# Graph attention and residual norm in float32: every product of the slots in four 64 by 64 tiles of TensorE, and the norms' statistics on ScalarE

## The chip, the cores and the metric

The kernel runs on one core of a Trainium2 chip. Its time is the device time of one execution in microseconds (us), the median of several runs. A core has a matrix engine (PE in the profile; PEld is its weight load), a vector engine (DVE), ScalarE (ACT), GpSimd (POOL) and SyncE (SP), which here issues most of the loads and stores. [...]

## The reference

Two layers on x of 8 batch elements, 2048 nodes and 256 features, with a symmetric 0/1 matrix adj of 2048 by 2048, four heads of 64.

```python
# layer 0
q, k, v = (x @ W.T + b, per head, for Wq, Wk, Wv)
scores = clip(q @ k.T / 8, -10, 10);  scores[adj == 0] = -10
attn = softmax over each chunk of 256 columns, 8 chunks        # not over all 2048
ctx = sum over the chunks of attn @ v
y = layernorm(ctx @ Wo.T + bo + x) * gamma + beta
x = layernorm(x + y)
# layer 1
Wh = x @ W;  e = leaky_relu(Wh @ a_src (rows) + Wh @ a_dst (columns), 0.2)
e[adj == 0] = -inf;  alpha = softmax(e) over all columns
x = layernorm(x + elu(alpha @ Wh))
```

All of it is in float32. There are three norms in an element: the inner norm of layer 0 (called a in the kernel), the outer one (b) and the one that closes layer 1 (c).

## The kernel before

Scores are made transposed, with columns j of the adjacency on the 128 partitions and 512 rows i along the free axis (CH = 512, so four groups q of rows). An element's layer 0 is cut into 64 **slots**: slot s is a group of rows q, a pair of heads hp and a chunk c of 256 columns. In a slot:

- `scores` makes four matmuls, for two blocks u of 128 columns and two heads k. Each head has 64 of the 128 rows of TensorE, so the two heads of a block run at once in two tiles of 64 by 128 (L385). They go to ps, two banks of PSUM in turn (`two_banks`, pool psA). DVE clips them and takes the mask, both in one instruction: the lesser of the score and the slab's byte, plus or minus 80 (L396). The slab is loaded three slots ahead.
- `exps`: ScalarE's exponential in place (L408).
- `product(s, k)`: for one head, attention times values, extended by a column of ones for the softmax's sum. One matmul is 128 rows by 64 columns of TensorE with 65 streamed columns (L422), and the two halves z of a block run at once in two column tiles. ScalarE copies the result out (L429).
- `normalize`: DVE's reciprocal (L437), GpSimd's multiply and add into acc (L444, L446).

While element b does layer 0, element b - 1 does **layer 1** in the same slots, in `Layer1.step`. The unit of layer 1 is half of the rows (BANKS = 8, 8 blocks of 128) and a head. A tile of it is 128 columns j by 1024 rows i: DVE makes e from the row factors srow, the column factor gd and the edge bytes et (`make`, L741), PE multiplies it into pa (`use`, L763, tiles of 128 by 64 again). A slot has two tiles (STEP = 2), made two ahead in three buffers.

The order on every engine is written out by hand (`manual_schedule`). In slot s, PE gets scores(s + 1), product(s, 0), layer 1's tiles, product(s, 1). DVE gets the reciprocal of slot s - 1, the clips of s + 1, then e. When a group of rows is finished, its output, two norms and projection to layer 1 (`Between`) are laid over the 16 slots of the next group by tables: AHEAD, BESIDE and BEHIND, and WIDE_... for the two middle groups. The number is the slot in the group; "beside" steps stand between the scores and the product, "behind" steps after the slot's work. `output` (L537) and `values` (L581, the projection, one block of 128 nodes at a time) are 128 by 128 matmuls, and they use a bank of their own, psM. The closing norm of element b - 2 (`Closing`) lies over the first 16 slots in the same way, and the last two elements have tables for the end, CLOSING_ALONE and ENDING.

```python
def stats(self, ks):                       # a norm's statistics, all on DVE
    for k in ks: nc.vector.bn_stats(...); nc.vector.bn_aggr(...)
    rs = var + EPS; off = -mean            # DVE
    rs = rs ** -0.5; off = off * rs        # GpSimd
def apply(self, dst):                      # ScalarE, L502
    dst = Identity(rs * src + off)         # four, of 256 columns
```

Between two elements stands a stretch in which the next element's x is projected to q, k and v (L329, L345) and the last group's `Between` is done in one go. `factors` then makes layer 1's row and column factors, and `rows` stores the row factors to rowD. After the last element, layer 1 runs alone (64 steps).

## Time and profile before

| | |
|---|---|
| median of 3 runs | 3774.59 us (3774.26 to 3775.82) |
| profiled execution | 3776.29 us, its span 3774.5 us |
| granted TensorE clock, mean | 0.993 of full speed |
| instructions in the span | 159,666 |
| DVE e (L741) | 1024 of 1286 ns |
| DVE pr (L396) | 1024 of 1207 ns |
| ACT exps (L408) | 1024 of 1055 ns |
| PE records of L422, L763, L385 | 32,768, 32,768, 4096 |

The page of the profile gives an engine's busy time, share of the span and instructions; then, for each line and operation, the tiles written and read, their shapes and count, the busy time, the mean duration and what the engine waited for before. "Busy" of a group is the time in which at least one of its instructions ran beyond the engine's earlier ones, so it is less than count times duration where they overlap. On PE every float32 matmul stands as two records, and each has a record of a weight load.

### The profile page before, as it was taken

To read this page: it belongs to the slowest core of one execution; us is meant where nothing else is said; L and a number is where in the kernel's file an instruction comes from. 1 tells how busy PE (TensorE), PEld (TensorE's weight loads), DVE (VectorE), ACT (ScalarE), POOL (GpSimd) and SP (SyncE) were. 2 spreads that over 40 slices of the span, in tenths; PEclk is the share of its full clock that TensorE was granted. 3 is DMA by queue.
4 is the path that set the end of the run, shared out by engine and by line. 5 is a ranking of instruction groups with operands and counts; after the bars stand their busy time and mean duration, and the time that the engine had idled before them with its cause. 6 is when DMAs were issued, how large, how long until landed. Compare 5 with 4: busy or idle time off the path is not lost.

```text
span 3774.5 us, 159666 instructions
## 1 busy us (share of the span) xinstructions
PE 3664.0 (97%) x72100; PEld 2741.3 (73%) x72100; DVE 3133.7 (83%) x4202; ACT 1988.0 (53%) x3665; POOL 1365.5 (36%) x1202
## 2 busy tenths in 40 slices
PE   9999999999999999999999999999999999999786
PEld 5656677776777777776777767777677777776676
DVE  5877489986999689895998959988699977988798
ACT  4666455555555555555555545555455555555322
POOL 1445234333433343333443324433334333334300
PEclk9999999999999999999999999999999999999998
DMA  6652333333333343333433334333433333433354
GB/s 163 152 117 69 78 98 109 105 75 112 106 108 105 86 119 102 104 93 88 133 97 98 100 89 135 109 100 78 113 107 107 105 80 112 115 97 84 95 154 128
DMA packets 672060, 398.46 MB, mean 106 GB/s; under 512 B 427280, under 2 KB 591504, under 8 KB 671376
## 3 DMA queue, kind: packets, MB, share of 16 engines
q1 hardware_dynamic: 621376, 354.54, 35.6%
q10 hardware_dynamic: 50000, 33.70, 2.8%
q8 instruction: 564, 9.24, 1.0%
q14 instruction: 120, 0.98, 0.1%
HBM read 331.22 MB, written 56.89 MB: 103 GB/s over the span
## 4 chain that ended last, share of the span: by engine, by line
PE 86%; DVE 5%; issue 3%; ACT 3%; DMA 1%; POOL 1%; SPq 0%; ACTq 0%; DVEq 0%; POOLq 0%
PE pc L422 26%; PE ps L385 24%; PE pa L763 22%; PE pp L329 5%; PE po L537 3%; PE pw L581 3%; PE pv L345 2%; DVE e L741 2%; ACT y L502 1%; DVE pr L396 1%; ACT pr L408 1%; DMA xp<-in_x_dram 0%; PE pm L246 0%; ACT qT L337 0%; SPq L279 0%
## 5 line engine op out<-in xcount | busy, mean ns | idle before, releaser
L396 DVE SCALAR_TENSOR_TENSOR pr<-ps,slab 128x1024 f32<-128x1024 f32 x1024 | 1194.3, 1207 | 211.1 <-PE ps L385 207.7
L422 PEld LDWEIGHTS pc<-vaug,pr 128*64 128x64 f32 x32768 | 1039.5, 138 | 406.4 <-issue 313.6
L741 DVE SCALAR_TENSOR_TENSOR e<-srow,gd,et 128x1024 f32<-128x1024 f32 x1024 | 1273.1, 1286 | 10.4 <-PE pa L763 5.8
L422 PE MATMUL pc<-vaug,pr 128*64 128x65 f32 x32768 | 1155.9, 224 | 14.3 <-ACT raw L429 7.7
L763 PE MATMUL pa<-waug,e 128*64 128x65 f32 x32768 | 1069.8, 224 | 41.0 <-DVE e L741 36.4
L763 PEld LDWEIGHTS pa<-waug,e 128*64 128x64 f32 x32768 | 1015.1, 139 | 60.1 <-DVE e L741 45.5
L408 ACT ACTIVATE pr<-pr 128x1024 f32<-128x1024 f32 x1024 | 1038.2, 1055 | 32.8 <-DVE pr L396 26.4
L385 PE MATMUL ps<-qT,kT 64*128 64x512 f32 x4096 | 1023.2, 616 | 3.5 <-DVE pr L396 2.9
L429 ACT COPY raw<-pc 128x260 f32<-128x260 f32 x1024 | 380.5, 372 | 1222.7 <-PE pc L422 1178.7
L444 POOL TENSOR_TENSOR part<-raw,rd 128x512 f32<-128x512 f32 x448 | 467.9, 1044 | 1407.5 <-DVE rd L437 1389.4
L446 POOL TENSOR_TENSOR acc<-acc,part 128x512 f32<-128x512 f32 x448 | 575.0, 1283 | 35.2
L385 PEld LDWEIGHTS ps<-qT,kT 64*128 64x128 f32 x4096 | 349.9, 186 | 326.6 <-issue 229.6
L437 DVE RECIPROCAL rd<-raw 128x8 f32<-128x8 f32 x512 | 100.8, 197 | 132.1 <-ACT raw L429 129.6
L444 POOL TENSOR_TENSOR acc<-raw,rd 128x512 f32<-128x512 f32 x64 | 66.7, 1043 | 339.3 <-DVE rd L437 339.3
L581 PE MATMUL pw<-w_sb,x1T 128*128 128x264 f32 x512 | 139.8, 409 | 6.1 <-DVE x1T L291 5.0
L795 ACT ACTIVATE sums<-sums,dn 128x64 f32<-128x64 f32 x512 | 134.0, 337 | 9.7 <-DVE dn L789 9.3
L497 POOL TENSOR_TENSOR rs_c<-rs_c,nhalf 128x4 f32<-128x4 f32 x32 | 54.0, 1687 | 223.8 <-DVE off_c L496 223.8
L537 PE MATMUL po<-wo_sb,qT 128*128 128x256 f32 x512 | 125.5, 390 | 3.1 <-DVE qT L464 2.8
L329 PE MATMUL pp<-xT,wk_sb 128*128 128x512 f32 x256 | 119.3, 609 | 7.9 <-ACT qT L337 6.6
L329 PE MATMUL pp<-xT,wq_sb 128*128 128x512 f32 x256 | 116.2, 597 | 0.0
L345 PE MATMUL pv<-wv_sb,xT 128*128 128x256 f32 x512 | 115.9, 379 | 0.0
L581 PEld LDWEIGHTS pw<-w_sb,x1T 128*128 128x128 f32 x512 | 92.4, 193 | 27.5 <-DVE x1T L291 5.3
(94 smaller groups left out, 1853.1 us busy)
## 6 DMA issues: line engine op xcount, KB each, us to landing
et<-edgeD SPq DMA_DIRECT2D x512, 256.0 KB, 3.1
slab<-clipD SPq DMA_DIRECT2D x512, 128.0 KB, 3.1
srow<-rowD SPq DMA_DIRECT2D x64, 512.0 KB, 5.0
xg<-in_x_dram SPq DMA_DIRECT2D x32, 512.0 KB, 5.3
x1D<-y ACTq DMA_DIRECT2D x32, 512.0 KB, 4.4
x1g<-x1D SPq DMA_DIRECT2D x32, 512.0 KB, 5.2
out_dram<-o SPq DMA_DIRECT2D x32, 512.0 KB, 3.3
ctxD<-acc ACTq DMA_DIRECT2D x56, 256.0 KB, 2.5
```

Source lines behind the costliest of these rows:

```text
L329: nc.tensor.matmul(pps[c], lhsT=w[:, kc, c * P : (c + 1) * P], rhs=st["xT"][:, kc, :], start=(kc == 0), stop=(kc == KC - 1),)
L385: nc.tensor.matmul(ps[:, k, :], lhsT=kT[rows, hp, t * P : (t + 1) * P], rhs=qT[rows, hp, cols], start=True, stop=True,)
L396: nc.vector.scalar_tensor_tensor(pr, pss[u], -CLIP, slab[:, u, :].unsqueeze(1).to_broadcast([P, 2, CH]), op0=ALU.max, op1=ALU.min,)
L408: nc.scalar.activation(pr, pr, AF.Exp, scale=0.125)
L422: nc.tensor.matmul(pc[z * D : (z + 1) * D, i, :], lhsT=probs[s][u][:, k, i * P + z * D : i * P + (z + 1) * D], rhs=vaug[:, KT * c + u, 2 * ...
L429: nc.scalar.copy(raws[s][:, k], pc)
L444: nc.gpsimd.tensor_mul(part, raw[:, :, :, :D], rd.to_broadcast([P, 2, QT, D]))
L446: nc.gpsimd.tensor_add(accv, accv, part)
L537: nc.tensor.matmul(po[:, k, :], lhsT=qT[:, c, t * P : (t + 1) * P], rhs=wo_sb[:, c, :], start=(c == 0), stop=(c == KC - 1),)
L581: nc.tensor.matmul(pw[:, k, : F + 2 * H], lhsT=self.x1T[:, c, u * P : (u + 1) * P], rhs=w1_sb[:, c, :], start=(c == 0), stop=(c == KC - 1),)
L741: nc.vector.scalar_tensor_tensor(e[:, :w], self.rows[n][:, :w], self.gd[:, h, j : j + 1], self.edge[k // JG][:, j % JG, :w], op0=ALU.max, ...
L763: nc.tensor.matmul(self.pa[i // QT][z * D : (z + 1) * D, i % QT, :], lhsT=e[:, i * P + z * D : i * P + (z + 1) * D], rhs=self.waug[:, j, h ...
```

## The change

The heads are put on the partitions differently. Values, layer 1's weights and probabilities now have 64 nodes on the partitions, twice: heads 0 and 1 on the lower half, heads 2 and 3 on the upper half. r says which half, v which head of it, and there are G = 32 groups of 64 nodes in place of 16 blocks of 128.

- A slot is now a group q, a half qh of its rows (256), a chunk c, and **all four heads**. The count of slots stays 64.
- Scores, product and layer 1's `use` are matmuls of 64 rows by 64 columns, in fours: r chooses the rows of TensorE (which heads), z its columns (which half of the output). The two r write to different banks.
- `product` is one call for all four heads, in 64 matmuls, followed by the exps of the next slot and then the copies (`keep`), so that layer 1 comes behind the whole product.
- Layer 1 goes by two heads at once, on 64 columns j. Its rows are cut into 6, 5 and 5 blocks, so a tile of e is 128 by 768 or 640, and an element has 192 of them. STEPS says how many a slot has. The tiles are made three ahead; the buffers stay three.
- clip and edge in DRAM have 64 partitions, and slab, edge and row loads come in two transfers, one for each half. A context is loaded in eight transfers for 256 rows of all heads, where before it was four for 512 rows of two heads.
- pv (projection of the values) and `Between.values` are 128 rows by 64 columns, in twos, to put the heads on their halves.
- psM is gone: psC has two banks, and output, values and small transposes use `two_banks`. The `add` of the output comes ahead of the slot's scores.
- The norms' sums and sums of squares are ScalarE's: four activations with an accumulated output for each, and GpSimd makes the mean and the factor. In the stretches between the elements and at the very end the old `stats` stays.

```diff
-    BANKS = (8, 8)
+    BANKS = (6, 5, 5)
+    G = N // D
+    KG = CHUNK // D
+    QH = CH // 2
+    QU = QH // P
-    QS = HP * NK
+    QS = 2 * NK
-    UNITS = [(m, h) for m in range(len(BANKS)) for h in range(H)]
+    UNITS = [(m, v) for m in range(len(BANKS)) for v in range(2)]
-    TILES = len(UNITS) * NT
+    TILES = len(UNITS) * G
     STEP = TILES // SLOTS
+    STEPS = (([3] * 10 + [2]) * 2 + [3] * 8 + [4] * 2) * 2
-    JG = 2
-    AHEAD_E = 3
+    JG = 4
+    AHEAD_E = 2
+    QUARTERS = [(r, z) for r in range(2) for z in range(2)]
+    HALF = [slice(0, D), slice(D, P)]
-    vaug = big.tile([P, NT, H, D1], F32, tag="vaug", name="vaug")
+    vaug = big.tile([P, G, 2, D1], F32, tag="vaug", name="vaug")
...
         def values():                       # of project
-            pv = two_banks([P, QT, F], "pv")
-            for u in range(QT):
+            pv = two_banks([P, 2 * QT, P], "pv")
+            for u in range(2 * QT):
                 for kc in range(KC):
-                    nc.tensor.matmul(
-                        pv[:, u, :],
-                        lhsT=st["xT"][:, kc, u * P : (u + 1) * P],
-                        rhs=wv_sb[:, kc, :],
+                    for r in range(HP):
+                        nc.tensor.matmul(
+                            pv[HALF[r], u, :],
+                            lhsT=st["xT"][:, kc, u * D : (u + 1) * D],
+                            rhs=wv_sb[:, kc, r * P : (r + 1) * P],
...
     def scores(s):
         for u in range(KT):
-            t = KT * c + u
             ps = two_banks([P, 2, CH], "ps")
-            for k in range(2):
-                rows = slice(k * D, (k + 1) * D)
-                nc.tensor.matmul(
-                    ps[:, k, :],
-                    lhsT=kT[rows, hp, t * P : (t + 1) * P],
-                    rhs=qT[rows, hp, cols],
+            for g in range(2):
+                j0 = (KG * c + 2 * u + g) * D
+                for r, z in QUARTERS:
+                    nc.tensor.matmul(
+                        ps[HALF[z], r, g * QH : (g + 1) * QH],
+                        lhsT=kT[HALF[r], z, j0 : j0 + D],
+                        rhs=qT[HALF[r], z, i0 : i0 + QH],
...
-    def product(s, k, alone):
+    def product(s):
+        pcs = [psC.tile([P, 2, QU, D1], F32, tag=f"psC{r}", name="pc") for r in range(2)]
+        for v in range(2):
+            for i in range(QU):
+                for k in range(KG):
+                    for r, z in QUARTERS:
+                        at = k % 2 * QH + i * P + z * D
+                        nc.tensor.matmul(
+                            pcs[r][HALF[z], v, i, :],
+                            lhsT=probs[s][k // 2][HALF[r], v, at : at + D],
+                            rhs=vaug[HALF[r], KG * c + k, v, :],
+                            start=(k == 0), stop=(k == KG - 1))
+    def keep(s, pcs):
+        for r, pc in enumerate(pcs):
+            nc.scalar.copy(raws[s][:, :, 2 * r : 2 * r + 2, :]..., pc)
...
     class Norm:
+        def total(self, func, where, **with_bias):
+            for k in range(QT):
+                junk = small.tile([P, F], F32, tag="ee", name="junk_" + self.name)
+                bias = {n: t[:, k : k + 1] for n, t in with_bias.items()}
+                nc.scalar.activation(
+                    junk, self.src[:, k, :], func, accum_out=where[:, k : k + 1], **bias)
+        def sums(self):
+            self.total(AF.Identity, self.off)
+            nc.gpsimd.tensor_scalar(self.off, self.off, -1.0 / F, None, ALU.mult)
+        def squares(self):
+            self.total(AF.Square, self.rs, bias=self.off)
+            nc.gpsimd.tensor_scalar(self.rs, self.rs, 1.0 / F, EPS, ALU.mult, ALU.add)
+            nc.gpsimd.tensor_tensor(self.rs, self.rs, nhalf, ALU.pow)
+            nc.gpsimd.tensor_mul(self.off, self.off, self.rs)
...
         def output(self, us):
-            if n == QT: po = two_banks([P, QT, F], "po")
-            else:       po = psM.tile([P, 2, F], F32, tag="psM", name="po")
+            po = two_banks([P, n, F], "po")
         def values(self, us):               # of Between
-            pw = psM or two_banks; per block of 128: 128 x 128 matmuls, 264 columns
+            pw = two_banks([P, 2 * n, QH], "pw")
+            for k in range(2 * n):
+                for c in range(KC):
+                    for r in range(HP):
+                        nc.tensor.matmul(
+                            pw[HALF[r], k, :W1],
+                            lhsT=self.x1T[:, c, node : node + D],
+                            rhs=w1_sb[:, c, r, :],
...
+    WIDE_AHEAD = {4: lambda o: o.add((0, 1)), 5: lambda o: o.add((2, 3))}
-    BESIDE: 4, 5 add; 5, 6 a.stats; 9, 10 b2.stats
+    BEHIND: 5 a.sums, 6 a.squares, 9 b2.sums, 10 b2.squares
-    WIDE_BESIDE: 4, 5 add; 6, 7 a.stats; 12, 13 b2.stats
+    WIDE_BEHIND: 5 a.sums, 6 a.squares, 11 b2.sums, 12 b2.squares
...
         def use(self):                      # of Layer1
             for i in range(BANKS[m]):
-                for z in range(2):
+                for r, z in QUARTERS:
                     nc.tensor.matmul(
-                        self.pa[i // QT][z * D : (z + 1) * D, i % QT, :],
-                        lhsT=e[:, i * P + z * D : i * P + (z + 1) * D],
-                        rhs=self.waug[:, j, h, :],
+                        self.pa[r][HALF[z], i, :],
+                        lhsT=e[HALF[r], i * P + z * D : i * P + (z + 1) * D],
+                        rhs=self.waug[HALF[r], j, h, :],
         def step(self):
             self.rest(1)
-            for _ in range(STEP):
+            for _ in range(STEPS[self.steps]):
                 self.make()
                 self.use()
+            self.steps += 1
...
-            product(s, 0, not lower)
+            pcs = product(s)
             if s + 1 < SLOTS:
                 for u in range(KT):
                     exps(s + 1, u)
+            keep(s, pcs)
             if lower:
                 if b + 1 < B or s < SLOTS - LATE:
                     lower.step()
-            product(s, 1, not lower)
```

The lines on the tables, on `output` and on `values` are shortened to what changes in them. CLOSING and CLOSING_ALONE get "sums" and "squares" where they had "stats", and ENDING moves the first closings of the last element to slots 25 to 31 and 46 to 52.

## Prediction

> **What bounds the kernel now.** I read the busy shares first, then the chain that ended last, then the slices of one batch element, then one slot in the timeline.

> ```profile
> PE 3664.0 (97%) x72100; PEld 2741.3 (73%) x72100; DVE 3133.7 (83%) x4202; ACT 1988.0 (53%) x3665; POOL 1365.5 (36%) x1202
> ...
> PE pc L422 26%; PE ps L385 24%; PE pa L763 22%; PE pp L329 5%; PE po L537 3%; PE pw L581 3%; PE pv L345 2%; DVE e L741 2%; ACT y L502 1%; DVE pr L396 1%; ACT pr L408 1%; DMA xp<-in_x_dram 0%; PE pm L246 0%; ACT qT L337 0%; SPq L279 0%
> ```

> PE is busy 97% of the span and makes 86% of the chain, 72% in three lines: scores (L385), product (L422), layer 1 (L763). The windows (start:end length, busy time of PE, PEld, DVE, ACT, POOL) of batch element 3, its four quarters of 16 slots (the last is one slot short) and the stretch up to the next element:

> ```profile
> 1335.50:1429.10 93.60, 93.07 (x2057) 69.67 (x2056) 89.63 (x125) 55.49 (x92) 40.09 (x36) 1.00 0.44 132
> 1429.10:1525.70 96.60, 96.60 (x2196) 74.91 (x2192) 90.40 (x115) 51.13 (x92) 39.37 (x34) 1.00 0.35 101
> 1525.70:1626.70 101.00, 101.00 (x2214) 77.63 (x2210) 91.34 (x116) 54.82 (x104) 39.29 (x34) 1.00 0.37 102
> 1626.70:1722.00 95.30, 95.30 (x2080) 73.15 (x2076) 87.69 (x112) 54.09 (x104) 36.94 (x32) 1.00 0.37 99
> 1722.00:1785.10 63.10, 61.39 (x450) 41.48 (x448) 24.04 (x48) 28.39 (x60) 15.02 (x14) 1.00 0.36 74
> ```

> PE is full in every quarter, while DVE is already at 92 to 96%: a faster PE has little room before DVE. One slot on PE (start, length, line, records):

> ```profile
> 1501.55 1.10 PE L422 MATMUL pc<-vaug,pr 128*64 128x65 f32 x32
> 1502.59 1.99 PE L385 MATMUL ps<-qT,kT 64*128 64x512 f32 x8
> 1504.50 1.15 PE L422 MATMUL pc<-vaug,pr 128*64 128x65 f32 x32
> 1505.48 2.04 PE L763 MATMUL pa<-waug,e 128*64 128x65 f32 x64
> 1507.35 1.10 PE L422 MATMUL pc<-vaug,pr 128*64 128x65 f32 x32
> 1508.38 1.99 PE L385 MATMUL ps<-qT,kT 64*128 64x512 f32 x8
> ```

> A float32 matmul is two records, each with a weight load, and two matmuls in different tiles run at once. L763's 64 records take 1.87 us from start to start: 58.4 ns for a pair of records. The score pairs stand 0.43 us apart in the trace. So the slot streams 4 x 0.429 + 16 x 2 x 0.0584 + 16 x 2 x 0.0584 = 5.45 us, and takes 5.79 from one L385 to the next. The other 0.34 us stands at the two seams where the tile shape changes: L422 to L385 (1.04 us for 0.93 of stream), in L385 (1.91 for 1.72) and at the start of the next L422 (0.98 for 0.93). Where L763 follows L422 in the same shape there is no such loss.

> [...]

> **The change part by part.**

> 1. Scores, product and layer 1 in one shape, 64 by 64. The seams in the slot go: -0.34 us. The streamed columns stay: a slot's product is 2 x 2 x 4 x 4 = 64 matmuls in 16 groups of four (before 32 in 16 pairs), and layer 1's three tiles of 5.33 blocks on average are 16 groups. If four tiles run at once as two do, a group record costs 58.4 ns again. Scores: 8 records-in-four of 256 columns, about 217 ns each (half of 429 and a few ns): 1.74 for 1.72 us. A plain slot is 1.74 + 1.87 + 1.87 = 5.48. PE's records double, from 72,100 to about 153,000. **The unknown price** is what a group of four costs in issue: 8 instructions every 58.4 ns, 7.3 each, where the trace sustains 14.6. Its lower bound is 54 ns of streaming (65 columns against 429 ns for 512), its upper bound is today's issue rate, 117 ns. I take 58.4, because weight load, matmul, weight load, matmul of a pair all start within 9 ns, which is 2 to 3 ns apiece.

> 2. Layer 1 in blocks of 6, 5, 5 columns of 128, 64 rows by two heads, not uniform over the slots. By the list of steps the quarters use 47, 49, 47 and 49 tiles, or 282, 262, 235 and 245 groups of 2 x 58.4 ns: 32.9, 30.6, 27.4, 28.6 us. With 27.8 for scores and 29.9 for products in each, 4.2 for two outputs (1.74 of stream and two seams, 0.35, each) in the last three, and 5.0 for four `values` in the last two (0.9 of stream and two seams, where one was before): PE needs 90.6, 92.5, 94.3, 95.5 = 373 us an element. Before, 93.6 + 96.6 + 101.0 + 101.1 (the last with its missing slot of 5.8) = 392. **PE alone would give 19 us an element.**

> 3. DVE. e goes from 1024 tiles of 1024 to 512 of 768 and 1024 of 640, the elements the same.

> ```profile
> L741 DVE SCALAR_TENSOR_TENSOR e<-srow,gd,et 128x1024 f32<-128x1024 f32 x1024 | 1273.1, 1286 | 10.4 <-PE pa L763 5.8
> 3588.60:3748.60 160.00, 135.72 (x3654) 120.76 (x3654) 139.15 (x116) 0.96 0.51 153
> ```

> In the last stretch (second line: PE and DVE on e alone), where DVE is never idle, one e costs 139.15 / 116 = 1.20 us; L548's adds of 512 and 1024 (680 and 1223 ns) give 1.06 ns an element, so 0.11 is fixed. That makes 0.93 and 0.79 to 0.80 us, or 43.9, 41.5, 37.6, 39.2 us a quarter against 38.4. Statistics leave DVE: 4 x 0.41 + 4 x 0.17 and small ones, 7.3 us in the first quarter (four closing norms, partly overlapped), 4.1 in the others. Unit ends and context turns in halves add about 1.1. DVE then needs 88.8, 90.6, 87.6, 90.8 us: below PE, at 93 to 98% of it. It was at 96% in the first quarter with PE full, so I charge only 4 us an element for waits between the two. One new tie: three tiles are made ahead with three buffers, so DVE writes an e only after PE's use in the same slot, and can't run ahead through the long slots.

> 4. ScalarE takes 8 activations a norm, 78 norms: 624 at about 0.59 us (row L502, 256 elements with two operand columns; bounds 0.37, a copy of 256, and 0.7) = 370 us, 1988 to 2360, 64%. They hide beside PE where a slot has room: ScalarE's base is 2 x 1.06 + 2 x 0.37 = 2.9 of 5.5 us, plus 2.4 for four of them, plus up to 2 for a unit's end. The exps of the next slot wait behind them and have some 2 us before the product needs them. Their scratch shares two buffers with layer 1's ee; where a unit's ee and a norm's sums fall in one slot (57 by the tables), ScalarE must wait for DVE's step in the next slot: about 1.5 us of PE an element. For the first element the buffers are shared with clip and its stores.

> 5. psM is gone: output, values and the small transposes take turns with the scores in psA, so each can hold a scores bank until DVE's add (moved ahead of the scores) or ScalarE's copy (0.37 + 0.18 us) is done. The first half of the scores (0.87 us) goes to the other bank and covers it; without that cover it is some 0.5 us for each of 6 places a group.

> 6. Stretches between elements: `values` now runs in 128 by 64 between lines of 128 by 128: seven places with two seams of 0.18: +2.5 us each, +20 over eight. Slabs, edges and rows come in two transfers of 64 partitions, contexts in eight for four: the bytes stay, SP issues some 1100 more at 0.3 to 0.4 us, about 2 of 5.5 us in a slot, with loads asked for two or three slots ahead: nothing. The instruction packets double to about 1200, one every 3.1 us and 1.9 in a run of product and layer 1; a fetch takes about 1 us: nothing, unless it waits long.

> 7. Last stretch, layer 1 alone on DVE: 64 x 0.93 + 128 x 0.80 = 162 against 154 us, less about 12 of statistics: -3.

> Sum: six elements x (19.4 - 4 - 1.5) = 83; the last, with 50 slots of layer 1, 9; the first 0 (30 slots without masks give 10, waits for the scratch take it); last slots of elements 3; between elements -20; end 3. Together **78 us off** 3776.3 (the profiled execution; its span is 3774.5, the median 3774.6): 3698, or **3696** on the median.

> **Rivals.**

> A. Issue. Four tiles can't be fed at 7.3 ns an instruction. 32,768 group records each cost more: at 10 ns an instruction 80 ns, +708 us: 4400. [...] At today's rate 117: 5620. It decides from 60.8 ns, 7.6 an instruction. For it: nothing here shows a denser stream than 14.6. Against: the starts within a pair. Slower.

> B. Coupling. PE's gain is given back because DVE at 98%, the shared psA turns and ScalarE's 2.4 us bursts stall it. It decides from 0.17 us a slot (78 / 448); at 0.25 us 3810. For it: DVE at 96% today. Against: PE was never idle beside that.

> C. The seams stay, because they come from waits or from the first weight load and not from the shape: 0.34 x 512 = 174 us more, 3870. Against: no seam between L422 and L763.

> **Numbers.** The forecast has 0.58, A 0.25, B 0.12, C 0.05. A measurement of this kernel tells about 0.2%, 7.5 us, from no change. The forecast's own range is 3625 (PE alone sets every quarter, no waits and no seams between elements) to 3775 (waits of 11 us an element on top); a few hundredths of it lie within 0.2%. Faster 0.55, same 0.05, slower 0.40. For eight in ten the range runs from 3620 into A up to 4150, some 72 ns a group record.

> **What would show it.** Right: slots of about 5.5 us, starts of four records within some 20 ns and 58 ns apart, no idle PE at L385's seams, DVE at 95% or more. Wrong: groups over 60 ns apart (A), PE waiting for DVE pr, DVE y or ACT pr by 0.2 us a slot (B), or 0.1 to 0.2 us lost at each change between the three lines (C).

## The result: 5119.34 us, 35.6% slower, and the profile after

The changed kernel takes 5119.34 us (median of 4 runs, 5109.22 to 5124.23), the kernel before 3775.2 (4 runs). The ratio is 1.3557, with a 95% interval of 1.3534 to 1.3581. The forecast was 3696 us. The profiled execution of the changed kernel took 5124.23 us, 1348 more than that of before.

The page of the changed kernel, in the order in which the page of before was read (busy time, share and count by engine; the queue that brings the instructions, in packets, MB and share; then the chain that ended last, by engine and by line):

```profile
PE 3875.3 (76%) x152996; PEld 3350.0 (65%) x152996; DVE 3142.4 (61%) x3998; ACT 2293.0 (45%) x4849; POOL 1390.0 (27%) x1342
...
q8 instruction: 1195, 19.58, 1.6%
...
PE 70%; issue 23%; ACT 3%; DVE 2%; DMA 1%; SPq 1%; ACTq 0%; DVEq 0%; POOL 0%; POOLq 0%
PE pa L834 22%; PE pc L454 20%; PE ps L421 18%; PE pp L358 3%; PE pw L643 3%; PE po L600 2%; PE pv L375 2%; ACT y L568 1%; SPq L308 1%; ACT pr L444 0%; DMA clipD<-clip 0%; ACT qT L366 0%; DVE e L812 0%; DVE pr L432 0%; DMA xp<-in_x_dram 0%
```

PE's busy time has grown little (3875 us for 3664), but it is 76% of the span in place of 97%. The three lines still lead the chain, and a new entry stands beside them: 23% "issue", time in which PE waited for nothing that the profile shows. Before it was 3%. The waits of PE (in total us, times, longest) say the same:

```profile
PE pa L834 <- issue: 764.0, 490, 3.8
PE pc L454 <- issue: 265.0, 293, 2.7
PE ps L421 <- issue: 74.1, 83, 2.4
PE pa L834 <- DVE e L812: 21.4, 7, 7.4
```

No other engine holds PE up for long: DVE makes e in 1385 us, and its idle time before e (1258 us) is ended by PE's pa. The windows of batch element 3 (start:end length; busy time of PE, PEld, DVE, ACT, POOL; clock, DMA share, GB/s) in the same quarters as before:

```profile
1745.90:1893.10 147.20, 103.47 (x4549) 93.51 (x4551) 89.23 (x100) 72.31 (x161) 40.08 (x42) 0.96 0.31 89
1893.10:2031.80 138.70, 101.97 (x4669) 93.75 (x4668) 90.79 (x112) 59.37 (x120) 41.11 (x38) 0.99 0.23 61
2031.80:2173.00 141.20, 107.72 (x4572) 94.69 (x4568) 90.57 (x114) 63.96 (x139) 39.65 (x38) 0.95 0.27 72
2173.00:2302.90 129.90, 98.47 (x4254) 84.83 (x4249) 85.77 (x106) 58.91 (x124) 36.98 (x36) 0.97 0.32 75
2302.90:2378.50 75.60, 65.32 (x1100) 47.14 (x1090) 26.68 (x54) 28.63 (x61) 16.82 (x13) 1.00 0.25 55
```

Each quarter lost 35 to 54 us. DVE does in 130 to 147 us the 86 to 91 us of work that it did in 94 to 101 before. Now one slot and a bit more on PE (start, length, line, records, idle before):

```profile
2491.41 1.84 PE L834 MATMUL pa<-waug,e 64*64 64x65 f32 x112
2495.01 0.63 PE L834 MATMUL pa<-waug,e 64*64 64x65 f32 x28 [1.75 <-issue]
...
2495.53 1.90 PE L421 MATMUL ps<-qT,kT 64*64 64x256 f32 x31
2497.19 1.17 PE L454 MATMUL pc<-vaug,pr 64*64 64x65 f32 x65
2499.30 1.10 PE L454 MATMUL pc<-vaug,pr 64*64 64x65 f32 x60 [0.94 <-issue]
...
2500.28 1.11 PE L834 MATMUL pa<-waug,e 64*64 64x65 f32 x64
2502.78 1.33 PE L834 MATMUL pa<-waug,e 64*64 64x65 f32 x76 [1.39 <-issue]
```

Two things can be read here. **In a burst the array does what the forecast said**: L834's 112 records start within 1.62 us (1.84 less the 0.22 of one record), 58 ns for each group of four. And **the bursts end in the middle of a run of the same instruction**, with no operand missing: 1.75, 0.94 and 1.39 us of nothing.

Where they end points to the cause. Number PE's instructions in order of time, weight loads and semaphore instructions included. Of 974 gaps of over half a microsecond between two starts, 868 then lie at one place of every 256. All gaps of over 150 ns at that place are 988, and make 1356 us together. The kernel before has 17 there, 5 us together, no more than at an average place. The page's instruction queue brings PE's program in packets of 16 KB, and PE's 2 x 152,996 records divided by 256 are 1195, which is the number of its packets. Before, 2 x 72,100 / 256 = 563 for 564. In the trace, at these pauses, a packet lands, PE goes on 1.39 us later, and the next packet starts 1.17 us after that (medians). Starts of packets are 3.79 us apart (median; 3.41 for the closest twentieth) and never under 3.26, though one is on its way for only 1.0 us.

### The profile page after: what moved, and what is told of

Read it like the earlier page. It is cut to its first block, busy times and chain, and to the rows that moved or that the text cites. A ratio compares the mean times of both kernels' runs of the same rounds, so it can differ in the third digit from the quotient of the medians.

```text
span 5121.6 us, 325190 instructions
## 1 busy us (share of the span) xinstructions
PE 3875.3 (76%) x152996; PEld 3350.0 (65%) x152996; DVE 3142.4 (61%) x3998; ACT 2293.0 (45%) x4849; POOL 1390.0 (27%) x1342
## 3 DMA queue, kind: packets, MB, share of 16 engines
q8 instruction: 1195, 19.58, 1.6%
## 4 chain that ended last, share of the span: by engine, by line
PE 70%; issue 23%; ACT 3%; DVE 2%; DMA 1%; SPq 1%; ACTq 0%; DVEq 0%; POOL 0%; POOLq 0%
PE pa L834 22%; PE pc L454 20%; PE ps L421 18%; PE pp L358 3%; PE pw L643 3%; PE po L600 2%; PE pv L375 2%; ACT y L568 1%; SPq L308 1%; ACT pr L444 0%; DMA clipD<-clip 0%; ACT qT L366 0%; DVE e L812 0%; DVE pr L432 0%; DMA xp<-in_x_dram 0%
## 5 line engine op out<-in xcount | busy, mean ns | idle before, releaser
L812 DVE SCALAR_TENSOR_TENSOR e<-srow,gd,et 128x640 f32<-128x640 f32 (+1 forms) x1536 | 1385.1, 937 | 1258.5 <-PE pa L834 1252.4
L834 PE MATMUL pa<-waug,e 64*64 64x65 f32 x65536 | 1255.0, 226 | 790.0 <-issue 764.0
L834 PEld LDWEIGHTS pa<-waug,e 64*64 64x64 f32 x65536 | 1141.8, 141 | 865.0 <-issue 837.4
L454 PE MATMUL pc<-vaug,pr 64*64 64x65 f32 x65536 | 1202.7, 220 | 287.8 <-issue 265.0
L454 PEld LDWEIGHTS pc<-vaug,pr 64*64 64x64 f32 x65536 | 1162.3, 136 | 376.6 <-issue 329.4
L421 PE MATMUL ps<-qT,kT 64*64 64x256 f32 x16384 | 1114.8, 395 | 89.8 <-issue 74.1
L421 PEld LDWEIGHTS ps<-qT,kT 64*64 64x64 f32 x16384 | 744.6, 139 | 275.3 <-issue 147.4
L643 PE MATMUL pw<-w_sb,x1T 128*64 128x132 f32 x2048 | 142.5, 288 | 9.2 <-DVE x1T L320 3.6
L643 PEld LDWEIGHTS pw<-w_sb,x1T 128*64 128x64 f32 x2048 | 118.6, 141 | 23.7 <-issue 14.4
L375 PEld LDWEIGHTS pv<-wv_sb,xT 128*64 128x64 f32 x2048 | 111.5, 137 | 23.0 <-ACT kT L366 12.8
```

The source lines that it names most:

```text
L421: nc.tensor.matmul(ps[HALF[z], r, g * QH : (g + 1) * QH], lhsT=kT[HALF[r], z, j0 : j0 + D], rhs=qT[HALF[r], z, i0 : i0 + QH], start=True, ...
L454: nc.tensor.matmul(pcs[r][HALF[z], v, i, :], lhsT=probs[s][k // 2][HALF[r], v, at : at + D], rhs=vaug[HALF[r], KG * c + k, v, :], start=(k ...
L643: nc.tensor.matmul(pw[HALF[r], k, :W1], lhsT=self.x1T[:, c, node : node + D], rhs=w1_sb[:, c, r, :], start=(c == 0), stop=(c == KC - 1),)
L812: nc.vector.scalar_tensor_tensor(e[:, :w], self.rows[n][:, :w], self.gd[:, h, j : j + 1], self.edge[k // JG][:, j % JG, :w], op0=ALU.max, ...
L834: nc.tensor.matmul(self.pa[r][HALF[z], i, :], lhsT=e[HALF[r], i * P + z * D : i * P + (z + 1) * D], rhs=self.waug[HALF[r], j, h, :], start ...
```

## The experiments

**Theory F** is instruction fetch: PE's program comes one block of 256 instructions at a time, not faster than one in 3.3 to 3.8 us (the closest and the median starts of packets above), or 13 to 15 ns an instruction. A slot's 576 instructions are 2.25 blocks, 8.5 us at 3.79. The slots of elements 1 to 6 take 549.7 us for 63, 8.7 each. The rivals were A and B of the prediction (each instruction costs its time in issue; waits between the engines), which the texts quoted below call theories I and W, and that loads compete with the fetch. Experiments 1, 2, 3 and 5 are one run each; in the last three the time moves by 1.7% or more, and the runs of the changed kernel differ by 0.3%.

**1. The array and its feed alone.** A small program: five stages of 512 groups on PE, with loads meant to run beside the last. The numbers are the tiles at once, the columns streamed, the groups and the loads.

```diff
+    stage("four65", 4, 65, 512)
+    stage("two65", 2, 65, 512)
+    stage("four33", 4, 33, 512)
+    stage("four130", 4, 130, 512)
+    stage("four65busy", 4, 65, 512, 32)
```

> TensorE alone, in five stages of 512 groups of float32 matmuls, each stage begun after a pause: four tiles of 64 by 64 with 65 streamed columns; two tiles of 128 by 64 with 65; four tiles with 33; four tiles with 130; four tiles with 65 beside 32 loads of 512 KB. Nothing of the reference is computed, the output is zero. Theory F (the instruction fetch: blocks of 256 instructions, one at a time, at least 3.3 us each): the first stage starts with some 400 to 600 instructions at 58 ns a group record and then averages 103 to 110 (8 instructions), in bursts with gaps of over 1 us; the second runs at 58 (a block then lasts 3.7 us); the third takes as long as the first, although half is streamed; the fourth 108 to 112, now by its streaming; the fifth 115 to 135, because the fetch shares the DMA engines. [...] Theory W (the four-tile products are as fast as the pairs, and the changed kernel loses by waits on the other engines): 58 ns in the first and fifth stage throughout.

Measured (604.44 us in all), ns for each group record on average: four tiles of 65 columns 134 in the first stage and 113 in the last, two tiles 60, four of 33 columns 116, four of 130 columns 120. The expectation had 103 to 110 for the first and 115 to 135 for the last. Part of the timeline of the first stage:

```profile
59.45 2.09 PE L64 MATMUL acc_four<-v_four,w_four 64*64 64x65 f32 x128 [1.74 <-issue]
63.18 2.09 PE L64 MATMUL acc_four<-v_four,w_four 64*64 64x65 f32 x128 [1.64 <-issue]
66.91 2.09 PE L64 MATMUL acc_four<-v_four,w_four 64*64 64x65 f32 x128 [1.64 <-issue]
70.64 2.09 PE L64 MATMUL acc_four<-v_four,w_four 64*64 64x65 f32 x128 [1.64 <-issue]
```

128 matmul records and their 128 weight loads, then 1.64 us of nothing, every 3.73 us, with no other engine, buffer or semaphore concerned. 130 columns stream for 109 ns (an estimate from the 429 ns of 512 columns in the kernel before); they cost little more than 65, 120 ns for the 113 of the last stage, and their pauses are never above 0.8 us: the stream fits into the fetch. Two tiles have half the instructions for the same columns and show a single pause, of 0.17 us. Rival A falls as it was put, since at the full clock the instructions of a block run at 7 ns apiece, 58 ns a group.

Two stages were not what they were built to be. PE stood at half of its clock for 108 of the 119 us of 33 columns, where a group takes 107 ns without any pause, so this average says nothing of the fetch. Fed at the full clock, a group of 33 columns takes 58 ns, as one of 65 does. And no load ran beside the last stage: the loads had been issued earlier, and the output's stores ran beside the first. PE's windows in the first stage with stores, with loads and with neither, and of the last stage (start:end length, busy time; clock, DMA share, GB/s):

```profile
9.00:49.00 40.00, 21.89 (x863) 0.66 1.04 341
56.00:100.00 44.00, 24.26 (x1496) 1.00 0.58 91
100.00:146.00 46.00, 25.83 (x1585) 1.00 0.02 4
483.60:599.20 115.60, 69.49 (x4095) 0.97 0.02 5
```

In the first of these, packets start 6.3 to 6.9 us apart, in the second 3.3 to 4.6, in the third 3.3 to 4.0. So the stores, at 341 GB/s, do slow the fetch. The clock was halved there for most of the time as well, but it still was from 53 to 56 us, where the queues were down to 111 GB/s and the next packet came after 3.36 us.

**2. Half of the streamed columns.** All matmuls but the first of each sum stream 33 of 65 columns; product and layer 1 get the same edit.

```diff
+                        f0 = 32 if k else 0
-                            rhs=vaug[HALF[r], KG * c + k, v, :],
+                            rhs=vaug[HALF[r], KG * c + k, v, f0:],
```

> The changed kernel with 33 in place of 65 streamed columns in product and layer 1, except in the first matmul of each accumulation; half of the features are left out of the sums. The instructions stay as many. Theory F: 5119 us becomes 5020 to 5140, since the streamed columns don't count. Theory I: the same. Theory W, or any in which the streaming in four tiles is the cost: 448 slots lose at least 1.3 us each, 4530 or less.

It took 5249.94 us, more than any theory expected. Halving the stream gained nothing. By itself that doesn't clear the array, since a group of 33 columns takes 58 ns in a run here too (median at the full clock). The extra 2.5% goes with the clock: it was halved for 1317 us of the span, for 345 in the changed kernel (mean granted clock 0.875 for 0.967). In the slots of elements 1 to 6, packets that start at the full clock are 3.77 us apart, for 3.75. Why the clock was halved more often isn't settled.

**3. Fewer instructions in layer 1.** Layer 1's matmuls of heads 2 and 3 (r = 1) are left out in all but the first and last tile of a unit.

```diff
                 for r, z in QUARTERS:
+                    if r and 0 < j < G - 1:
+                        continue
```

> The changed kernel without the upper half's matmuls of layer 1 (heads 2 and 3), except for the first and last tile of a unit: 32,768 x 0.94 / 2 fewer matmuls, about 60,000 of 306,000 instructions less. DVE and ScalarE do what they did, the four tiles become two in layer 1. Theory F: 60,000 / 256 = 236 blocks fewer at 3.8 to 4.0 us: 900 to 940 us less, 4180 to 4250; a little more where PE's own work then shows. Theory W: within 2% of 5119, since the other engines' work and the streaming time of a group stay.

4456.03 us. The packets fall from 1195 to 956, the time by 663 us: 2.8 us for each block saved. The direction is F's; the size is below the forecast of 900 to 940. The pauses at the block boundaries fall by 774 us, from 1356 to 582, and the time by less, so something else fills a part of what they leave.

**4. The statistics, both ways.** In the changed kernel they go back to DVE:

```diff
         def sums(self):
+            return
...
         def squares(self):
+            self.stats(tuple(range(QT)))
```

> The changed kernel with the norms' statistics back on DVE (in the place where ScalarE's squares stood). Theory F: within 0.6% of 5119; the statistics lie beside a PE that waits for instructions. Theory W: if ScalarE's bursts cost, 2% or more less; if DVE were the limit, 3% or more longer.

In the kernel before, ScalarE's statistics are put in alone:

```diff
-        5: [lambda o: o.add((2, 3)), lambda o: o.a.stats((0, 1))],
-        6: [lambda o: o.a.stats((2, 3)), lambda o: o.shift()],
+        5: [lambda o: o.add((2, 3))],
+        6: [lambda o: o.shift()],
...
+        5: lambda o: o.a.sums(),
+        6: lambda o: o.a.squares(),
```

> The kernel before with nothing changed but the norms' statistics, which ScalarE takes (behind the slots' work, as in the changed kernel). TensorE sets the slots there and is never idle in them, so all theories expect no change that can be measured, 3766 to 3784 us; ScalarE rises by about 370 us and DVE falls by about 200. Over 3800 would say that ScalarE's bursts of four stall the exponentials.

The changed kernel with DVE's statistics takes 5135.35 us, ratio 1.3611 (1.3588 to 1.3634); the kernel before with ScalarE's takes 3786.56, ratio 1.0026 (1.0016 to 1.0037), just above what a measurement can tell. The other tables of the old kernel are changed in the same way (not shown). The place of the statistics is worth 0.3% in either direction.

**5. Without the loads of masks and edges.** Slab and edge tiles are loaded once and kept.

```diff
+        if kept:
+            slab_of[s] = kept[0]
+            return
...
+                if kept_edge:
+                    self.edge[k] = kept_edge[0]
+                    return
```

> The changed kernel with one slab and one block of edges loaded once and kept: every slot uses the same masks, and some 250 MB of loads are gone. Theory F with a fetch that shares the DMA engines: the blocks come every 3.4 to 3.6 us where they came every 3.8 in the middle, and the time falls to 4600 to 4900. Theory F with a fetch that takes its own time whatever else is moved: 5050 to 5130.

5030.68 us, 1.7% less, a little below the range of a fetch that takes its own time (5050 to 5130) and far above that of one that shares (4600 to 4900). The queues move 38 GB/s for 77, and packets start 3.76 us apart for 3.79. At the rates of this kernel the loads are not what holds the fetch up. They are not without effect: where PE waited for two packets in turn, these started 3.53 us apart in the changed kernel while the DMA engines were under 10% busy with other transfers, and 4.1 above 70% (medians).

**6. Two of the four tiles, everything else kept.** In product and layer 1 only two of the four tiles are fed (z = 0), except in the first group of a sum and, in layer 1, the last. PE has 36% fewer instructions. The groups, their stream, the schedule, the other engines' work, buffers and DMAs stay.

```diff
+                        if z and k:
+                            continue
...
+                    if z and 0 < j < G - 1:
+                        continue
```

> The changed kernel with only two of the four tiles (z = 0, both r) in product and layer 1, except in the first step of an accumulation (and the last of layer 1): half of the rows are left out of the sums, the groups and their streaming time stay, and DVE, ScalarE, GpSimd, the transfers, the bank turns and the schedule are those of the changed kernel. About 360 instead of 576 instructions a slot. Theory F: 1.4 blocks a slot at 3.7 us are 5.2 us, below the 5.5 that the streaming takes, so the time is what the prediction's other steps give, 3696 us, or up to 3850 where the bursts of product and layer 1 (300 instructions in 3.7 us) outrun the fetch. Theory W: within 3% of 5119, since every wait between the engines stays.

3893.22 us, ratio 1.0309 (1.0294 to 1.0325): 1226 us gone with the instructions alone, and 764 packets for 1195. It is 43 us above the range expected. Its page (by engine; the queue) and its windows of element 3:

```profile
PE 3627.4 (93%) x97700; PEld 3197.0 (82%) x97700; DVE 3176.3 (82%) x3998; ACT 2262.0 (58%) x4849; POOL 1436.3 (37%) x1342
...
q8 instruction: 764, 12.52, 1.4%
```

```profile
1390.00:1487.60 97.60, 93.11 (x2845) 85.86 (x2845) 89.19 (x99) 68.59 (x157) 39.70 (x42) 1.00 0.43 119
1487.60:1585.90 98.30, 95.39 (x2904) 88.87 (x2901) 94.38 (x113) 60.02 (x124) 42.27 (x39) 1.00 0.36 95
```

PE and DVE are both back at 91 to 97% of their quarters. Waits between engines (rival B) would have stayed. This run also comes near to what the change would have been without the fetch: 75 us of pauses at the boundaries are left in it.

**7. Half-size tiles in the kernel before.** The cleanest test leaves the old kernel as it was and only cuts its column tiles in two: product and layer 1 in four tiles of 128 by 32 (528 instructions a slot for 272), then the product alone (400).

```diff
-                for z in range(2):
+                for z in range(4):
-                        pc[z * D : (z + 1) * D, i, :],
+                        pc[z * SQ : (z + 1) * SQ, i, :],
```

(SQ is 32; `use` gets the same in the first kernel.)

> The kernel before with the products and layer 1 in four column tiles of 128 by 32 in place of two of 128 by 64, and nothing else: layouts, order, buffers, transfers, other engines' work and streamed columns stay, PE's instructions in a slot go from 272 to 528. Theory F: a slot of layer 0 with layer 1 needs 528 / 256 = 2.06 blocks at 3.7 to 4.0 us, 7.6 to 8.3 us in place of 5.8 to 6.3, and the last stretch 3.4 us for a step where DVE needs 2.5: 4550 to 4950 us, with PE's gaps at one place in every block of 256. Any theory that puts the changed kernel's loss on its new layout, on psM, on the transfers in halves or on ScalarE: within 1% of 3775.

> The same in the products alone; layer 1 keeps two tiles. 400 instructions a slot, 1.56 blocks. Theory F: 5.8 to 6.2 us a slot against the 5.8 that PE works, so this is about where the fetch begins to count: 3775 to 3980, and most of it in the plain slots. Theory F's rivals: within 1% of 3775.

Both cut: 4890.13 us, ratio 1.2975 (1.2924 to 1.3027). The layout, the schedule and all other engines are those of before, and five sixths of the loss are there (1115 of 1344 us), with pauses at the block boundaries of 1144 us in the profiled execution (4931 us). Its page and its timeline:

```profile
q8 instruction: 1075, 17.61, 1.5%
...
PE 74%; issue 20%; DVE 2%; ACT 2%; DMA 1%; SPq 0%; POOL 0%; ACTq 0%; DVEq 0%; POOLq 0%
```

```profile
2002.03 0.71 PE L422 MATMUL pc<-vaug,pr 128*32 128x65 f32 x33
2004.42 0.66 PE L422 MATMUL pc<-vaug,pr 128*32 128x65 f32 x30 [1.68 <-issue]
...
2010.75 0.52 PE L422 MATMUL pc<-vaug,pr 128*32 128x65 f32 x22
2012.73 0.84 PE L422 MATMUL pc<-vaug,pr 128*32 128x65 f32 x42 [1.47 <-issue]
```

The product alone: 4078.79 us, ratio 1.081 (1.0777 to 1.0844), above the range expected. 400 instructions at 3.4 to 3.8 us a block are 5.3 to 5.9 us, about the slot's 5.8, and a slot isn't even: 190 us of boundary pauses were found. The other 110 us or so fit two more seams a slot, which the expectation had left out: product and layer 1 now differ in tile shape, and starts at that change stand 150 ns apart (52 before).

**8. Edges further ahead.** The run of experiment 6 with edge tiles of two blocks, five ahead in six buffers, since its end had waited for edge loads.

```diff
-    JG = 4
-    AHEAD_E = 2
+    JG = 2
+    AHEAD_E = 5
```

> The kernel of the run with two of four tiles (half of the rows left out of the sums), with the edges of layer 1 loaded in blocks of two tiles, five blocks ahead in six buffers, where it is blocks of four, two ahead in three buffers: the same memory, but the loads are asked for ten tiles ahead and a buffer comes free after two tiles. That run's last stretch is 305 us, 38 more than before, with edge loads on its chain four times. If the short lead of the edges is the cause, the last stretch falls to 270 to 285 and the time from 3893 to 3855 to 3875; if the ScalarE statistics of the closing norms are (their chain through GpSimd, and scratch shared with layer 1), it stays at 300 to 310 and the time within 8 us of 3893.

3895.45 us, ratio 1.0319 (1.0301 to 1.0336): no change, the last stretch is 302 us for 305. The edges' lead isn't what makes it long. The expectation gives this outcome to ScalarE's statistics; but in the kernel before (experiment 4) they lengthen the last stretch only from 267 us to 271, so its cause stays open.

No version here beats the kernel before.

## Why the prediction was wrong, point by point

**The step that failed is in step 6**: "The instruction packets double to about 1200, one every 3.1 us and 1.9 in a run of product and layer 1; a fetch takes about 1 us: nothing, unless it waits long." The count was right (1195 packets), and so was the need of one in 1.9 us where PE is fed. But this need was set against the time that a packet is on its way, 1.0 us, as if fetches could follow one another. They don't: no kernel here has two starts closer than 3.2 us. A need of one in 1.9 us can't be met, and PE waits at the end of most blocks (988 of 1196). The pauses make 1356 us, about the size of the whole loss of 1348. The two needn't agree, since other waits hide behind the pauses; what fewer instructions take away is 1226 us (experiment 6). The trace of before held the warning: no two of its 564 packets start within 3.31 us of each other, with a median of 5.74. Nor do the fetches run ahead where PE leaves them time: in nine of ten cases a packet starts between 1.5 us before and 2.3 us after PE begins the block of the same number. So each fetch keeps step with PE, and the three medians of the changed kernel, 1.0, 1.39 and 1.17 us, add up to a round of 3.6. The trace of before showed no faster rate than that, so the unknown should have been bounded by 3.31 us, as the price of a group was bounded by today's issue rate. Little is held ahead, too: in the two stages of experiment 1 with four tiles of 65 columns the first pause came after 446 and 186 instructions. And the fetch is hidden only while instructions are some 14 ns apart or more: at 15 ns (60 / 4, the two tiles of experiment 1) there was one pause of 0.17 us, at 7 ns one after each block in the timeline of the four.

**Rival A** had the direction, and the result lies between two of its prices (4400 us at 80 ns a group, 5620 at 117), but for another reason. The instructions of a block are issued at 7 ns apiece (a group in 58 ns); what is slow is the coming of the next block. 3.79 us for 256 is 118 ns for a group's eight instructions, A's highest price, 117. The kernel did not reach A's 5620; scores, with 27 ns an instruction (a group of L421 in 216 ns, median), and the stretches between elements (2190 records in 75.6 us behind element 3, a block in 8.8) need fewer blocks than can come, which is likely why. In the trace of before the two matmuls of a pair already start 7 ns apart (median).

**Step 1, the array: right.** Groups of four run at 58 ns where they are fed, and no seam is left: from L454 to L834 starts are 7 ns apart, from L834 to L421 39 (medians), where before the change of shape from L422 to L385 took 152. Rival C is out.

**Steps 2 and 3, the slots: near in experiment 6**, as far as two tiles can stand for four. Elements 1 to 6 take 384.8 us for 63 slots (386.4 before), with 8 to 11 us of pauses left in them; the forecast was about 373 (378.5 less one slot), which is nearly met if the pauses are taken off. e starts every 0.80 and 0.93 us in the last stretch, as priced. Rival B, 0.17 us a slot, did not come.

**Steps 4 and 5** were not what decided: 0.3% for the statistics (experiment 4), and in the slots of experiment 6 the turns in psA cost nothing that shows.

**Three terms of the sum were mis-sized**, seen in experiment 6 (+116 us on before: slots -10, last element -3, and the following):

- First element, 0 in the forecast, took 344 us for 306: +38. DVE's waits in it (us, times, longest) show the masks' way through DRAM, which the kernel before didn't wait for. PE's longest waits in it are for ScalarE's copy of a product (22.8 us).

```profile
DVE clip L270 <- DMA clipD<-clip: 16.4, 10, 3.6
DVE pr L432 <- DMA slab<-clipD: 13.3, 12, 3.8
```

- Stretches between elements, +2.5 each in the forecast, took 71 us for 63. The seams were priced, psA wasn't: without psM, output and values take turns with the projections, and PE now waits for copies of the bank before. Behind element 3, four such waits are 4.2 us, before one of 0.9; two of the four in the timeline of PE:

```profile
1837.40 3.70 PE L358 MATMUL pp<-xT,wk_sb 128*128 128x512 f32 x8 [1.05 <-ACT qT L366]
...
1842.45 3.71 PE L375 MATMUL pv<-wv_sb,xT 128*64 128x128 f32 x64 [1.25 <-ACT kT L366]
```

- The end, -3 in the forecast, took 305 us for 267: +38. DVE's work in it is what it was (241 us for 236), its idle time doubled (64 for 31). Of the 64 us idle, 23 stand at the ends of layer 1's units, where 10 stood before (groups, with count, busy and mean, idle before and its releaser):

```profile
L881 DVE SCALAR_TENSOR_TENSOR h<-ee,sums 128x320 f32<-128x320 f32 (+1 forms) x16 | 7.4, 503 | 12.0 <-ACT sums L877 12.0
...
L863 DVE TENSOR_SCALAR dn<-sums 128x10 f32<-128x10 f32 (+1 forms) x8 | 1.4, 170 | 11.4 <-ACT sums L850 11.4
```

These three causes are read from the trace of that run; none was taken away by itself, and the edges' lead, tried for the end, is cleared. Even with the remaining 75 us of pauses taken off in full, an estimate, experiment 6 would stand at about 3818 us, 1% slower than before. What stays open besides is why the clock fell in experiment 2, and whether four tiles pay with fewer instructions a slot. It would have to be few: 400 a slot left 190 us of pauses (experiment 7), 360 left 75 (experiment 6).

## What to carry to other kernels

Before cutting matmuls into more and smaller tiles, count PE's instructions in the densest stage (a float32 matmul is two records and two weight loads in these traces) and set them against the fetch: 256 instructions in 3.4 to 3.8 us here, about 14 ns each, where the array, once fed, ran them at 7, and 6.3 to 6.9 us beside stores of 341 GB/s. A row of "issue" pauses in the middle of a run of one instruction, at one place of every 256, was the mark of it here (868 of 974 gaps of over half a microsecond). Issuing less helped (663 us in experiment 3, 1226 in experiment 6). And where a trace shows no faster rate of something than the change needs, bound it by the fastest that it shows, not by how long one takes.
